# A decoder layer's experts: the down product of four chunks in seven block products instead of eight

## The chip, the cores and the metric

The kernel runs on one core of one Trainium2 chip. The metric is the device time of one execution in microseconds, less is better. Everything is float32 unless said otherwise. The engines are named as the profile names them: PE (TensorE, matrix products), PEld (its weight loads), DVE (VectorE), ACT (ScalarE), POOL (GpSimd) and SP (SyncE, which here only starts DMA transfers).

## The reference, cut to what matters

One decoder layer on x of 4 x 512 tokens and 512 features: attention with 32 query heads, then a product with a quantized context, then a feed-forward part with 8 experts, each step added to x. The change concerns the experts. Each takes its 256 tokens (C) and computes

```python
# E = 8 experts, C = 4*512/8 = 256 tokens each, D = 512, H = 704
h  = silu(einsum('ecd,edh->ech', xd, W1)) * einsum('ecd,edh->ech', xd, W3)
oe = einsum('ech,ehd->ecd', h, W2)          # the "down" product
out = take(oe, ...) * gate                   # rows back to their tokens
return out + silu(xt @ sw1) * (xt @ sw3) @ sw2   # plus a shared expert
```

## The kernel before, in words

The program runs attention, the context product and the shared expert's first part under a planner that mixes jobs between the heads. After that the order is written out by hand: a loop over the 8 experts (L1524), then the last four pieces of the shared expert's down product, with the gathers of the experts' rows and the final additions between them (L1572 to L1591). The change lies in the expert loop and in what it leaves in memory for the end.

H = 704 is cut into five chunks of 128 (HF = 5) and a half chunk of 64. The activations of an expert lie transposed, with H on the partitions, in egTs[e] (the profile calls it slot_s, since it lies in the space of the shared expert's first weights). gT[:, c, :] is chunk c for all 256 tokens, in two tiles of 128 tokens.

One pass of the loop, for expert e:

- Five calls of up7, one for each chunk c. up7 computes the two input products of the chunk at once, as 2 x 2 blocks in seven products (Strassen, in Winograd's form), each of two matmuls 128 x 128 x 128. The products go to PSUM banks, six to the tag "sp" (4 banks, in turn) and product 3 to "av" (1 bank). DVE adds them up (L1345 to L1360), ACT applies Silu (L1359), and POOL makes the last multiplication g = g * c2 (L1361). So a chunk of gT is finished by POOL.
- After each up7, weight_sums puts four additions or subtractions for the next expert's weights on POOL (L1307 to L1310). They are instructions of 256 elements per partition through the helper on L279, as all of POOL's are. After chunk 1 the rows of expert e + 1 are turned (PE and ACT), and after chunk 2 expert_sums puts its four token sums on POOL.
- expert_rest(e + 1): the half chunk of the next expert (one sp bank, L1216, L1231 to L1235).
- down: for each of the two token tiles one bank of tag "mm" (3 banks), a matmul with the half chunk (L1242) and five with the whole chunks (L1253), 512 columns each. With late=True chunk 4 comes last. DVE copies each bank to yo (L1540), and SP writes it to oe.
- Loads on SP in between: rows, weights of expert e + 2, its W2 once down is through (load_w2).

Each engine takes its instructions in the order in which the program issues them. A bank or a buffer is reused in turn: an instruction that writes it waits until the one that read it last is through. c2 and u2 have two buffers each.

Rows of x2 (x after the first two steps) are brought back for the final additions: rows_back (L1519) takes places from a list spare, which starts with the four chunks of h3x[B - 1], the last input of the shared expert, no longer needed. At expert 5 four rows come back into the first four places, and six by xtile into buffers of their own; at expert 7 six more come into places of spare:

```python
    spare = [h3x[B - 1][:, k, :] for k in range(KC)]
        if e == E - 1:
            rows_back(first[2:])
        if e == E - 3:
            rows_back(tiles[0] + first[:2])
            for i in tiles[1] + tiles[2] + tiles[3]:
                xtile(i)
```

## Time and profile before

| what | value |
| --- | --- |
| median of 3 runs | 1563.4 us (1562.38 to 1567.21) |
| profiled execution, its own time | 1567.81 us |
| its span, first to last instruction | 1566.1 us |
| mean granted clock of PE | 0.993 |
| PE busy in the span | 1535.0 us (98%) |
| DVE, ACT, POOL busy | 920.8, 537.4, 544.9 us |
| start of expert 0's first matmul of up7 to the end of expert 7's down | about 1301 to 1523 us |

The profile is of one execution, with times in microseconds from the start of the span. "Busy" of PE includes modelled ends of pipelined matmuls, so two matmuls in a row can overlap in it; the distance of their starts is what one costs. In a timeline line the columns are the start, the duration, the engine, the line of the program, the operation with output and inputs, their sizes and the count; a bracket at the end tells how long the engine stood idle before and what it waited for. In a table by windows the columns are the window, its length, the busy time of PE, PEld, DVE, ACT and POOL with the number of instructions, the granted clock of PE, the DMA share and GB/s. The chain of waits goes back from the last instruction, each step to what released it. A float32 matmul appears as two PE instructions, so the 80 matmuls of the experts' whole chunks are 160 rows on L1253.

### The profile page before, as it was taken

The numbers are of one execution on the slowest core, as the hardware profiler recorded it, in microseconds if no ns is written. First come the engines' busy times: TensorE is split into PE (matmuls) and PEld (weight loads), VectorE is DVE, ScalarE is ACT, GpSimd is POOL, SyncE is SP. The second block draws the span as 40 slices with busy tenths as digits, with TensorE's granted clock in tenths as the row PEclk, the third lists the DMA queues.
The fourth block names the chain that finished last, engine by engine and source line by source line (L and its number), as shares of the span: only waits on it lengthen the run. The fifth ranks groups of instructions, "written<-read, shape, count | busy, mean of one in ns | idle before, by whom it ended". The sixth has DMA issues, their size and how long they took to land.

```text
span 1566.1 us, 22168 instructions
## 1 busy us (share of the span) xinstructions
PE 1535.0 (98%) x7325; PEld 895.8 (57%) x7325; DVE 920.8 (59%) x2732; ACT 537.4 (34%) x1615; POOL 544.9 (35%) x568
## 2 busy tenths in 40 slices
PE   9999999999999999999999999999999999999999
PEld 5455555545545545554555545554446778877864
DVE  4466843467776575887656485665655554434434
ACT  3344443434433434443444444552101121111100
POOL 2131211203334121333312133143535148776723
PEclk9999999999999999999999999999999999999999
DMA  4473431534234344423425342246041234665616
GB/s 150 128 229 133 101 102 28 155 101 102 82 81 142 87 125 135 106 84 79 144 86 131 112 122 62 61 149 202 14 176 68 83 140 147 202 206 200 214 68 215
DMA packets 118227, 193.90 MB, mean 124 GB/s; under 512 B 17120, under 2 KB 36832, under 8 KB 117600
## 3 DMA queue, kind: packets, MB, share of 16 engines
q10 hardware_dynamic: 65216, 100.42, 21.7%
q1 hardware_dynamic: 50336, 83.67, 17.3%
q0 software_dynamic: 2560, 8.39, 1.5%
q8 instruction: 58, 0.95, 0.3%
q14 instruction: 57, 0.47, 0.1%
HBM read 135.54 MB, written 27.53 MB: 104 GB/s over the span
## 4 chain that ended last, share of the span: by engine, by line
PE 86%; DVE 4%; DMA 3%; issue 2%; ACT 2%; POOL 2%; SPq 0%; ACTq 0%; POOLq 0%; DVEq 0%
PE py L414 14%; PE psq L314 13%; PE sc L945 9%; PE av L1026 8%; PE p_e L1336 8%; PE pt L995 8%; PE p_s L1336 5%; PE epy L1253 4%; PE psv L356 4%; PE ys L1253 4%; PE psk L314 3%; ACT pm L978 1%; PE p_s L1216 1%; PE p_e L1216 1%; PE ptr_h L263 1%
## 5 line engine op out<-in xcount | busy, mean ns | idle before, releaser
L978 ACT ACTIVATE pm<-pm,mn 128x256 f32<-128x256 f32 (+3 forms) x512 | 280.9, 550 | 381.8 <-DVE mn L968 356.8
L968 DVE CUSTOM_DVE_ANT_0 pm<-sc,mask 128x256 f32<-128x256 f32 (+3 forms) x512 | 216.6, 485 | 91.6 <-PE sc L945 91.6
L414 PE MATMUL py<-wo,aT 128*128 128x512 f32 x512 | 239.9, 602 | 3.3 <-issue 2.0
L314 PE MATMUL psq<-hT,wq 128*128 128x512 f32 x512 | 236.5, 599 | 2.3 <-DVE y L610 2.3
L279 POOL TENSOR_TENSOR t1q<-t1q,tsq 128x512 f32<-128x512 f32 x64 | 84.2, 1316 | 396.5 <-DMA tsq<-t2q 221.6
L1012 DVE COPY pT<-pt 128x128 f32<-128x128 f32 (+3 forms) x256 | 114.2, 485 | 113.9 <-PE pt L995 105.5
L945 PE MATMUL sc<-kT,t1q 64*128 64x384 f32 (+3 forms) x1024 | 166.7, 450 | 7.3 <-ACT pT L1006 2.5
L995 PEld LDWEIGHTS pt<-ident,pm 128*128 128x128 f32 x1280 | 144.2, 141 | 37.0 <-issue 28.1
L995 PE MATMUL pt<-ident,pm 128*128 128x128 f32 x1280 | 154.9, 274 | 0.3 <-DVE mn L968 0.2
L1026 PE MATMUL av<-pT,v 128*64 128x512 f32 (+3 forms) x1024 | 153.0, 440 | 1.7 <-ACT pT L1006 1.7
L314 PEld LDWEIGHTS psq<-hT,wq 128*128 128x128 f32 x512 | 91.9, 190 | 102.1 <-issue 96.4
L414 PEld LDWEIGHTS py<-wo,aT 128*128 128x128 f32 x512 | 92.1, 190 | 97.2 <-issue 89.2
L1006 ACT COPY pT<-pt 128x128 f32<-128x128 f32 (+3 forms) x256 | 97.1, 430 | 146.6 <-PE pt L995 118.6
L945 PEld LDWEIGHTS sc<-kT,t1q 64*128 64x128 f32 x1024 | 84.5, 187 | 88.5 <-issue 55.6
L279 POOL TENSOR_TENSOR acc<-acc,y 128x512 f32<-128x512 f32 x64 | 81.1, 1271 | 153.5 <-DVE y L610 152.0
L1026 PEld LDWEIGHTS av<-pT,v 128*64 128x64 f32 x1024 | 68.5, 137 | 109.3 <-issue 97.2
L978 ACT ACTIVATION_READ_ACCUMULATOR pm<-pm,mn 128x1 f32 x512 | 95.5, 186 | 0.0
L279 POOL TENSOR_TENSOR aT<-aT,rrb 128x512 f32<-128x512 f32 x64 | 81.8, 1308 | 23.6 <-DMA rrb<-rrd 23.6
L422 DVE TENSOR_TENSOR acc<-py,acc 128x512 f32<-128x512 f32 x64 | 43.8, 686 | 47.3 <-PE py L414 47.0
L1253 PE MATMUL epy<-slot_e,slot_s 128*128 128x512 f32 x160 | 70.8, 597 | 0.0
L323 DVE TENSOR_TENSOR t2q<-psq,rt 128x512 f32<-128x512 f32 x64 | 44.0, 688 | 43.3 <-PE psq L314 40.8
L1253 PE MATMUL ys<-slot_s,gT 128*128 128x512 f32 x140 | 64.4, 610 | 0.0
(245 smaller groups left out, 2078.4 us busy)
## 6 DMA issues: line engine op xcount, KB each, us to landing
slot_e<-in_L_ffn_W_dram SPq DMA_DIRECT2D x14, 1280.0 KB, 8.6
wq<-in_L_attn_wq_dram ACTq DMA_DIRECT2D x16, 1024.0 KB, 6.5
tsq<-t2q SPq DMA_DIRECT2D x256, 64.0 KB, 2.1
wo<-in_L_attn_wo_dram ACTq DMA_DIRECT2D x16, 1024.0 KB, 5.3
rrb<-rrd ACTq DMA_DIRECT2D x32, 512.0 KB, 7.4
slot_e<-in_L_ffn_W_dram SPq DMA_DIRECT2D x7, 1408.0 KB, 6.2
kT<-t1k ACTq DMA_DIRECT2D x64, 128.0 KB, 2.8
wk<-in_L_attn_wk_dram ACTq DMA_DIRECT2D x16, 256.0 KB, 2.9
```

Source lines behind the costliest of these rows:

```text
L279: nc.gpsimd.tensor_tensor(*args)
L314: nc.tensor.matmul(ps, w[:, k, c0 : c0 + P], hTs[b][:, k, :], start=(k == 0), stop=(k == KC - 1),)
L414: nc.tensor.matmul(py, aT[:, r, j * P : (j + 1) * P], wts["o", a][:, r, :], start=(r == 0), stop=(r == 3),)
L945: nc.tensor.matmul(scs[g][:, o : o + nk], qTs[b, p][g * HD : (g + 1) * HD, it * P : nk], kTs[b, p // 2][g * HD : (g + 1) * HD, 0:nk], star ...
L968: nc.vector.tensor_tensor_reduce(out=pm[:, o : o + nk], in0=scs[g][:, o : o + nk], in1=mask[:, T - nk : T], scale=-(HD**-0.5), scalar=3.0e ...
L978: nc.scalar.activation(pm[:, o : o + nk], pm[:, o : o + nk], AF.Exp, bias=mn, scale=-1.0, accum_out=rss[b, a][:, col : col + 1],)
L995: nc.tensor.transpose(pt[:, j * P : (j + 1) * P], pms[g][:, j * P : (j + 1) * P], ident)
L1006: nc.scalar.copy(pT[:, 0 : it + 1, it * P : nk], pt[:, o : o + nk].rearrange("p (j t) -> p j t", t=P),)
L1012: nc.vector.tensor_copy(pT[:, it + 1, 0:nk], pt[:, o : o + nk])
L1026: nc.tensor.matmul(av[g * HD : (g + 1) * HD, j * P : T], vs[b][:, j, v0 : v0 + HD], rhs, start=(j == 0), stop=(j == TB - 1),)
L1253: nc.tensor.matmul(pys[i], gT[:, c, (t + i) * P : (t + i + 1) * P], w2[:, c, :], start=False, stop=(c == HF - 1),)
L1336: nc.tensor.matmul(ps, w[:, k, :], x[:, k, :], start=k == 0, stop=k == 1)
```

## The change

Chunks 0 to 3 of the down product become a 2 x 2 block product: the activations in blocks of (token tile) x (two chunks), W2 in blocks of (two chunks) x (256 columns). Seven products of two matmuls with 256 columns take the place of eight matmuls with 512 columns. The half chunk and chunk 4 stay as they were.

- down_sums: four subtractions on w2 (512 elements per partition each), by DVE, two after chunk 1 and two after chunk 2 of the same expert. The results lie in three chunks of h3x[B - 1]; one replaces a block of w2.
- inner_sums: four additions or subtractions on gT (256 elements each), by DVE. One is issued after chunk 3, three inside up7 of chunk 4, at the second call of mid, which lies between L1352 and L1357 of before. One replaces a block of gT; two results lie in the fourth chunk of h3x[B - 1], one in a tile s4 of its own.
- down7: products 0 to 2 go to sp banks and product 3 to the av bank; products 4 to 6 are added to the mm banks by PE itself. ACT copies product 0, DVE makes four sums of 256 elements, and these are added to the banks where before yo was copied.
- spare no longer holds h3x[B - 1], but four buffers of rows (xes) instead. All ten rows that rows_back brings come at expert 7.

Lines from up7 on are 74 higher in the changed kernel. The whole diff but for blank lines:

```diff
--- before.py
+++ after.py
@@ -1261,6 +1261,80 @@
                 mid()
         return pys
+    def down_sums(w2, ts, which=range(4)):
+        b11, b12, b21, b22 = (
+            w2[:, k : k + 2, c : c + D // 2] for k in (0, 2) for c in (0, D // 2)
+        )
+        t1, t2, t4 = ts
+        todo = (t1, b12, b11), (b12, b22, b12), (t2, b22, t1), (t4, b21, t2)
+        for n in which:
+            nc.vector.tensor_tensor(*todo[n], ALU.subtract)
+        return t1, t2, b12, t4, b11, b21, b22
+    def inner_sums(gT, t, ss, which):
+        a11, a12, a21, a22 = (
+            gT[:, k : k + 2, j * P : (j + 1) * P] for j in (t, t + 1) for k in (0, 2)
+        )
+        s2, s3, s4 = ss
+        todo = (
+            (s3, a11, a21, ALU.subtract), (a21, a21, a22, ALU.add),
+            (s2, a21, a11, ALU.subtract), (s4, a12, s2, ALU.subtract),
+        )
+        for n in which:
+            nc.vector.tensor_tensor(*todo[n])
+        return a11, a12, a21, a22, s2, s3, s4
+    def down7(gT, w2, t, inner, sums, name, tag):
+        a11, a12, s1, a22, s2, s3, s4 = inner
+        t1, t2, t3, t4, b11, b21, b22 = sums
+        half = D // 2
+        pys = [bank(tag, f"{name}_{i}") for i in range(2)]
+        for i, py in enumerate(pys):
+            nc.tensor.matmul(
+                py,
+                gT[i * HT : (i + 1) * HT, HF, (t + i) * P : (t + i + 1) * P],
+                w2[i * HT : (i + 1) * HT, HF, :],
+                start=True,
+                stop=False,
+            )
+        def product(i, a, b, ps=None):
+            first = ps is None
+            if first:
+                ps = bank("av" if i == 3 else "sp", f"d7_{name}_{i}")[:, 0:half]
+            for k in range(2):
+                nc.tensor.matmul(
+                    ps, a[:, k, :], b[:, k, :], start=first and k == 0, stop=first and k == 1
+                )
+            return ps
+        def part(tag, n):
+            return gp.tile([P, n], F32, tag=tag, bufs=2, name=f"d{tag}_{name}")
+        u2, lo, hi = part("u2", half), part("c2", D), part("c2", D)
+        nc.scalar.copy(lo[:, 0:half], product(0, a11, b11))
+        nc.vector.tensor_tensor(u2, product(1, s2, t2), lo[:, 0:half], ALU.add)
+        nc.vector.tensor_tensor(hi[:, 0:half], product(2, s3, t3), u2, ALU.add)
+        p5 = product(3, s1, t1)
+        nc.vector.tensor_tensor(lo[:, half:D], p5, u2, ALU.add)
+        nc.vector.tensor_tensor(hi[:, half:D], p5, hi[:, 0:half], ALU.add)
+        product(4, a12, b21, pys[0][:, 0:half])
+        product(5, s4, b22, pys[0][:, half:D])
+        product(6, a22, t4, pys[1][:, 0:half])
+        for i, (py, more) in enumerate(zip(pys, (lo, hi))):
+            nc.tensor.matmul(
+                py,
+                gT[:, HF - 1, (t + i) * P : (t + i + 1) * P],
+                w2[:, HF - 1, :],
+                start=False,
+                stop=True,
+            )
+            yield py, more
     def down_last(gT, w2, t, name):
         parts = [(0, 0, D), (1, 0, D // 2), (1, D // 2, D)]
@@ -1512,7 +1586,9 @@
     for pair in tiles:
         kept.update(pair)
     first = [i for i in range(NT) if i not in kept]
-    spare = [h3x[B - 1][:, k, :] for k in range(KC)]
+    spare = []
     spare += [xSs.rearrange("p i k t -> p (i k t)")[:, k * D : (k + 1) * D] for k in range(4)]
     spare += [wS_flat[:, k * D : (k + 1) * D] for k in range(NHC * CAP // D)]
@@ -1521,9 +1597,23 @@
             xts[i] = spare.pop(0)
             nc.sync.dma_start(out=xts[i], in_=x2[i * P : (i + 1) * P, :])
+    h3v = h3x[B - 1]
+    ts = [h3v[:, k, :].rearrange("p (k c) -> p k c", k=2) for k in range(3)]
+    ss = [h3v[:, 3, k * 2 * P : (k + 1) * 2 * P].rearrange("p (k t) -> p k t", k=2) for k in range(2)]
+    s4 = ep.tile([P, 2, P], F32, name="s4")
+    ss.append(s4)
     for e in range(E):
         for c in range(HF):
-            up7(evw[e][0], exS[e], egTs[e][:, c, :], c, CAP, f"e{e}_{c}")
+            def mid(ns=0, room=0, calls=[]):
+                calls.append(room)
+                if c == HF - 1 and len(calls) == 2:
+                    inner_sums(egTs[e], 0, ss, (1, 2, 3))
+            up7(evw[e][0], exS[e], egTs[e][:, c, :], c, CAP, f"e{e}_{c}", mid)
+            if c in (1, 2):
+                down_sums(evw[e][1], ts, (0, 1) if c == 1 else (2, 3))
+            if c == 3:
+                inner_sums(egTs[e], 0, ss, (0,))
             if e < E - 1:
                 weight_sums(evw[e + 1][0], c)
             if c == 1:
@@ -1534,16 +1624,17 @@
         expert_rest(e + 1)
         load_e(e + 2)
         if e == E - 1:
-            rows_back(first[2:])
-        for t, py in enumerate(down(egTs[e], evw[e][1], 0, f"epy_{e}", "mm", late=True)):
+            spare.extend(xes[e, t] for t in range(CT) for e in (E - 2, E - 1))
+            rows_back(tiles[0] + first)
+        inner, sums = inner_sums(egTs[e], 0, ss, ()), down_sums(evw[e][1], ts, ())
+        for t, (py, more) in enumerate(down7(egTs[e], evw[e][1], 0, inner, sums, f"epy_{e}", "mm")):
             yo = ep.tile([P, D], F32, tag="yo", bufs=2, name=f"yo_{e}_{t}")
-            nc.vector.tensor_copy(yo, py)
+            nc.vector.tensor_tensor(yo, py, more, ALU.add)
             r0 = e * CAP + t * P
             nc.sync.dma_start(out=oe[r0 : r0 + P, :], in_=yo)
         load_w2(e + 2)
         if e == E - 3:
-            rows_back(tiles[0] + first[:2])
             for i in tiles[1] + tiles[2] + tiles[3]:
                 xtile(i)
```

## The prediction

> **What bounds the kernel now.** I read the page's busy shares first, then the chain that ended last, then the timeline of one expert. Expert 4 stands for all; in what follows *t* is the time in us after its first matmul at 1413.63.

> ```profile
> PE 1535.0 (98%) x7325; PEld 895.8 (57%) x7325; DVE 920.8 (59%) x2732; ACT 537.4 (34%) x1615; POOL 544.9 (35%) x568
> ```

> ```profile
> 1405.01 8.78 PE epy L1253 x20
> 1413.79 6.25 PE p_e L1336 x56
> 1420.91 9.38 PE p_e L1336 x84
> 1433.08 8.78 PE epy L1253 x20
> 1441.86 6.25 PE p_e L1336 x56
> ```

> The chain through the experts consists of PE's matmuls alone, one expert each 28.07 us (1441.86 - 1413.79). So a matmul less is time gained, and anything that keeps PE waiting is time lost. DVE has slack here (14.6 to 18.3 us busy in 40). POOL has less: the timeline shows it in one unbroken run of 29 instructions from t=4.05 (1417.68) to t=25.9, and late against the others:

> ```profile
> 1429.48 0.28 DVE L1352 TENSOR_TENSOR slot_s<-p_e,p_e 128x128 f32<-128x128 f32 x1
> ...
> 1429.88 0.29 DVE L1357 TENSOR_TENSOR slot_s<-p_e,u_e 128x128 f32<-128x128 f32 x1
> ...
> 1431.22 0.73 POOL L279 TENSOR_TENSOR xS<-h3x,xS 128x256 f32<-128x256 f32 x1
> 1431.91 0.73 POOL L279 TENSOR_TENSOR slot_s<-slot_s,c_e 128x256 f32<-128x256 f32 x1
> 1431.95 1.13 PE L1242 MATMUL epy<-slot_e,slot_s 64*128 64x512 f32 x4
> ...
> 1432.59 0.73 POOL L279 TENSOR_TENSOR wS<-slot_e 128x256 f32<-128x256 f32 x1
> ```

> The slot_s product at 1431.91 is the one that finishes chunk 3 of gT (t=18.3 to 19.0). DVE is by then through chunk 4 (L1352 at t=15.9, L1357 at t=16.3). Before the change nobody suffers: `down` takes chunk 3 as its fourth matmul.

> [...]

> ```profile
> 1261.06 0.68 DVE L1320 TENSOR_TENSOR xS<-h3x 128x512 f32<-128x512 f32 x1
> 1261.66 1.75 DVE L1320 TENSOR_TENSOR xS<-h3x,xS 128x512 f32<-128x512 f32 x1
> ...
> 1261.17 1.70 POOL L279 TENSOR_TENSOR gT<-gT,c_s 128x512 f32<-128x512 f32 x1 [7.59 <-DVE xS L1320]
> ```

> POOL takes 1.70 instead of its usual 1.31; the last DVE subtraction takes 1.75 instead of 0.69 and ends 0.54 after POOL does. [...]

> ```profile
> 1283.85 1.94 PE L263 MATMUL ptr_e<-ident,xe 128*128 128x128 f32 x8 [3.21 <-DMA xe<-xd]
> ...
> 1283.00:1286.00 3.00, 2.15 (x9) 2.10 (x10) 0.00 (x0) 0.76 (x2) 2.84 (x5) 0.50 0.92 312
> 1286.00:1289.00 3.00, 3.00 (x9) 2.37 (x7) 0.00 (x0) 0.79 (x2) 2.92 (x4) 0.50 1.02 375
> 1289.00:1292.00 3.00, 3.00 (x14) 2.63 (x13) 1.60 (x4) 0.00 (x0) 2.77 (x5) 0.92 1.04 371
> ```

> The seventh figure after the window is the clock (the five bracketed busy times come first). A wait of 3.21 us was followed by 5.6 us of work at half clock (1283.85 to 1289.5), 2.8 us lost. The other long PE waits: 3.08 us at 1163.9 cost (1170.0 - 1167.0)/2 = 1.5 us; waits of 2.00 (586) and 1.47 (352 and 1134) were also each followed by 3.4 us at 0.50; 1.70 (1070) and 1.37 (914) were not.

> **The change part by part.**

> *Matmuls removed.* A 128x512 matmul is two PE instructions 0.427 apart (20 take 8.78 with their tail). Those of 128x256 with the same kind of operands (p_s, L1336) start 0.865 apart in fours, 0.216 each. Per expert 16 instructions of 0.427 (6.83) become 28 of 0.216 (6.03): **-0.80 us**, eight times. The half chunk (L1242) and chunk 4 stay. Weight loads of 0.19 remain under 0.216.

> *Sums of w2 (T1 to T4).* Four DVE instructions of 512 elements, both inputs in SBUF, two after chunk 1 (t=6.7) and two after chunk 2 (t=10.7). Alone 0.69 each; but POOL is in its run, so they alternate with it. At 376 to 383 four POOL products (usual 1.27) alternate with DVE's L460 and L462, which take 1.64 each and start 1.68 apart: a DVE instruction takes 1.68 - 1.27 = 0.41 from POOL. So T1 to T4 make POOL late by 4 x 0.41 = 1.64. DVE itself: two of them behind a POOL instruction each last about 2 us; chunk 2's L1345 (t=8.3) comes 0.5 late, chunk 3's (t=11.4) 1.2 late, at 12.65 to 12.95. It frees the bank of product 1 for product 6 (six `sp` banks' worth per chunk on four banks), due at t=12.8: PE waits about **0.2**. Bounds 0 and 1.

> *Sums of gT.* S3 after chunk 3: 256 elements, alone 0.42, takes 0.15 more from POOL. S1, S2, S4 stand in DVE's queue between L1352 and L1357 of chunk 4, at t=16.2, and S1 needs POOL's product of chunk 3. That now ends at 19.0 + 1.64 + 0.15 = 20.8. POOL goes straight on with its weight sums; S1, S2 and S4 each get in behind one of them. The hold of a 256 POOL instruction is about 0.60 (0.73 less the 0.13 to 0.15 by which the other starts before its end), that of a DVE one 0.27 (half the 0.54 above). S1 starts at 21.4 and ends at 21.85, S2 at 22.7, S4 at 23.6; L1357 and its semaphore end at 23.95.

> *Who waits.* Behind these three on DVE: L1357 and L1360 of chunk 4, the two of `expert_rest` (L1234, L1235) and the first sums of `down7`; behind L1357 on ACT: the Silu of chunk 4, that of the rest and the copy of product 0. On PE: product 1 needs S2 and the bank that L1357 frees (chunk 4's products 4, 5, 6 and the rest fill all four; product 0 takes the one that L1352 freed). PE comes to it at t = 19.4 (start of L1253 now) + 0.2 + 0.86 (product 0) = 20.45. It waits until 23.95: **+3.5**. Bounds: no sharing of the port at all gives 19.0 + 3 x 0.42 + 0.29 = 20.6, a wait of 0.2; a full POOL instruction and a full DVE one per step (1.15 instead of 0.87), and the upper end for the T sums, gives about 4.8.

> *Clock.* A wait of 3.5 is of the kind that led to half clock both times (3.08, 3.21): (1.5 + 2.8)/2 = **+2.1**. Bounds 0 and 2.8.

> *The rest of down7.* `hi` takes the c2 buffer of chunk 4, so its first sum waits for POOL's product of chunk 4 (24.4 to 25.1: after Silu at 24.35); PE ends product 2 at 25.7, so that is covered. The ACT copy ends near 25. Three more DVE sums of 0.42 lie under products 4 to 6 (2.6 us) and chunk 4 (1.7 us). yo's addition reads PSUM and SBUF at the price of the copy (0.69 for 128x512, as L1396): nothing. If the cover goes, each costs 0.4.

> *Rows.* Four loads of x2 (256 KB each) move from expert 5 to expert 7 on SP, 10 instead of 6 ahead of the writes of yo; at 0.43 each to issue from 1512.4 they are out by 1517, and yo comes at 1523. If transfers lag, the gathers (1527 to 1547) shift by at most 2 to 3; the DVE work behind them is over some 6 us before PE needs a bank. Nothing, at most 2. Of POOL's and ACT's queues only the copy is new.

> *Sum.* Experts 0 to 6: -0.80 + 0.2 + 3.5 + 2.1 = +5.0 each. Expert 7 has no weight sums on POOL (its chunk 3 is ready 1 us before S1 is issued): -0.8. Total 7 x 5.0 - 0.8 = +34.2. The profiled run took 1567.8 (span 1566.1), 4.4 above the median of 1563.4; the difference is laid on the median: **1597.6**, rounded 1597.

> **The rivals.** *Clock kept*: the wait comes[...]. 7 x (0.2 + 3.5 - 0.8) - 0.8 = +19.5: 1583. For it: one wait of 1.70 left the clock alone; against: both above 3 did not. *The port costs nothing (ends faster)*: 256-element instructions slip into the gaps of 0.08 between POOL's (0.73 long, 0.81 apart in part), POOL isn't pushed back, S1 starts at 19.05 and PE waits 0.2: 8 x -0.8 + 7 x 0.2 = -5.0: 1558. It decides where product 1 can start before t = 19.4 + 0.86 + 0.8 = 21.05; later than that the saving is gone. [...] *Worse*: the upper bounds together, 7 x (-0.8 + 0.2 + 4.8 + 2.8) - 0.8 = +48: 1612. That the matmuls are not saved is excluded: 14 of 256 columns stand for 8 of 512 in the program.

> **How the numbers follow.** Stall and half clock 0.60 (1588 to 1607), clock kept 0.18 (1573 to 1588), free port 0.15 (1556 to 1564), worse 0.07. The range 1570 to 1612 leaves out the free port and half of the worst. About 0.3% (4.7 us) is what a measurement of this kernel can tell from no change: the free port splits into 0.08 faster and 0.07 within; the rest, 0.85, is slower.

> **What would show it.** Right: PE idle of 3 to 4 us per expert ahead of product 1, released by DVE; S1's line idle for POOL; DVE's subtractions of 512 at 1.0 or more instead of 0.69; POOL's product of chunk 3 near t=20.8; a clock of 0.50 for 3 us or more after it; expert 7 faster by 0.8. Wrong: S1, S2, S4 at 0.42 back to back, PE idle below 0.5 per expert, or a period of the experts under 28.

## The result, and the profile after

The changed kernel takes **1583.99 us** (median of 5 runs, 1580.02 to 1587.52) where the kernel before takes 1564.04 (5 runs, 1562.38 to 1567.21): ratio **1.0129** (95% interval 1.0115 to 1.0144), 20 us slower. The profiled execution took 1580.02 with a span of 1578.2. The predicted 1597 is 13 us too high: the direction, the place and the wait behind POOL are as predicted, the half clock behind that wait is not.

The page of after, its busy times and the shares of the chain that ended last; below them the shares of before:

```profile
PE 1531.1 (97%) x7421; PEld 914.5 (58%) x7421; DVE 983.0 (62%) x2828; ACT 539.1 (34%) x1623; POOL 557.6 (35%) x568
...
PE 79%; POOL 8%; DVE 6%; DMA 3%; issue 2%; ACT 2%; SPq 0%; ACTq 0%; POOLq 0%; DVEq 0%
```

```profile
PE 86%; DVE 4%; DMA 3%; issue 2%; ACT 2%; POOL 2%; SPq 0%; ACTq 0%; POOLq 0%; DVEq 0%
```

PE has less work and still the program takes longer. The chain tells why: before, PE held 86% of it and POOL and DVE 6%; now these two hold 14%. POOL has as many instructions as before (568) and 12.7 us more of busy time: they are the same operations, and those that run beside DVE's new ones are slower (next to the second pair of w2 sums 1.06 and 1.17 us instead of 0.73).

What the chain passes through in one expert, the fourth (the chain of after, start, length, what). The experts are numbered from 0, so this is expert 3:

```profile
1387.41 5.82 PE p_e L1410 x52
...
1404.05 0.69 POOL xS L279
1404.74 0.07 issue
1404.81 0.79 POOL xS L279 x2
1405.60 0.58 issue
1406.18 0.72 POOL xS L279
1406.90 0.69 POOL slot_s L279
1407.60 0.02 issue
1407.62 0.94 DVE slot_s L1286
1408.56 0.02 issue
1408.58 0.84 DVE h3x L1286
1409.42 0.02 issue
1409.45 0.83 DVE s L1286
1410.28 0.21 DVE slot_s L1431
1410.49 0.04 issue
1410.53 2.86 PE d_epy L1310 x12
```

Read it from below. Product 1 of down7 (L1310, 1410.53) starts when DVE's L1431 has freed its bank. L1431 stands in DVE's queue behind S1, S2 and S4 (the three L1286). S1 starts when POOL has finished chunk 3 of gT (the slot_s of L279, 1406.90). And that multiplication comes at the end of POOL's run, right behind four token sums for the next expert (xS), which nobody needs yet.

What PE and DVE wait for there (timeline of after):

```profile
1406.86 0.73 POOL L279 TENSOR_TENSOR slot_s<-slot_s,c_e 128x256 f32<-128x256 f32 x1
1407.47 1.13 PE L1310 MATMUL d_epy<-slot_e,slot_s 128*128 128x256 f32 x4
1407.62 0.93 DVE L1286 TENSOR_TENSOR slot_s<-slot_s 128x256 f32<-128x256 f32 x1 [3.44 <-POOL slot_s L279]
1408.35 0.78 POOL L279 TENSOR_TENSOR slot_e<-slot_e 128x256 f32<-128x256 f32 x1
1408.58 0.83 DVE L1286 TENSOR_TENSOR h3x<-slot_s 128x256 f32<-128x256 f32 x1
1409.21 0.79 POOL L279 TENSOR_TENSOR wS<-slot_e 128x256 f32<-128x256 f32 x1
1409.45 0.83 DVE L1286 TENSOR_TENSOR s<-slot_s,h3x 128x256 f32<-128x256 f32 x1
...
1410.20 0.28 DVE L1431 TENSOR_TENSOR slot_s<-p_e,u_e 128x128 f32<-128x128 f32 x1
1410.53 1.13 PE L1310 MATMUL d_epy<-h3x 128*128 128x256 f32 x4 [1.93 <-DVE slot_s L1431]
```

DVE stood idle for 3.44 us with its next work behind S1; S1, S2 and S4 take 0.93, 0.83 and 0.83 instead of the 0.41 to 0.42 of such a sum alone, in strict turn with POOL; and PE waits 1.93 for product 1.

An expert as a whole, expert 4 before and expert 3 after, from its first matmul to the next expert's (windows: length, then busy time and count of PE, PEld, DVE, ACT and POOL, clock, DMA share, GB/s):

```profile
1413.63:1441.70 28.07, 28.07 (x181) 22.04 (x180) 11.42 (x40) 4.77 (x13) 20.58 (x29) 1.00 0.58 198
```

```profile
1387.25:1417.53 30.28, 28.02 (x193) 24.39 (x192) 19.54 (x52) 5.03 (x14) 22.43 (x29) 1.00 0.57 183
```

In what follows the length of such a window is called the period: 28.07 before, 30.28 after (30.40 in expert 0, 32.01 in expert 4); for expert 7, which prepares nothing, 25.56 before and 25.39 after. The loop takes 222.1 us before (1301.33 to 1523.41) and 239.2 after (1296.28 to 1535.50), 17.1 more. The end of the program behind it is 42.7 us in both. Ahead of the loop, where the program is the same, the two executions differ by 5 us the other way, so their own times (1567.81 and 1580.02) show only 12.2 of it.

### The profile page after: what moved, and what is told of

It reads as the page before. It is cut to its first block, busy times and chain, and to the rows that moved or that the text cites. A ratio compares the mean times of both kernels' runs of the same rounds, so it can differ in the third digit from the quotient of the medians.

```text
span 1578.2 us, 22472 instructions
## 1 busy us (share of the span) xinstructions
PE 1531.1 (97%) x7421; PEld 914.5 (58%) x7421; DVE 983.0 (62%) x2828; ACT 539.1 (34%) x1623; POOL 557.6 (35%) x568
## 4 chain that ended last, share of the span: by engine, by line
PE 79%; POOL 8%; DVE 6%; DMA 3%; issue 2%; ACT 2%; SPq 0%; ACTq 0%; POOLq 0%; DVEq 0%
PE py L414 14%; PE psq L314 13%; PE sc L945 9%; PE av L1026 8%; PE pt L995 8%; PE p_s L1410 5%; PE psv L356 4%; PE ys L1253 3%; PE psk L314 3%; PE p_e L1410 3%; POOL wS L279 3%; PE d_epy L1310 2%; POOL slot_s L279 1%; PE epy L1310 1%; PE p_s L1216 1%
## 5 line engine op out<-in xcount | busy, mean ns | idle before, releaser
L279 POOL TENSOR_TENSOR t1q<-t1q,tsq 128x512 f32<-128x512 f32 x64 | 83.8, 1310 | 395.8 <-DMA tsq<-t2q 241.7
L279 POOL TENSOR_TENSOR acc<-acc,y 128x512 f32<-128x512 f32 x64 | 81.1, 1272 | 151.3 <-DVE y L610 149.8
L279 POOL TENSOR_TENSOR aT<-aT,rrb 128x512 f32<-128x512 f32 x64 | 81.9, 1312 | 25.3 <-DMA rrb<-rrd 25.3
L610 DVE TENSOR_TENSOR y<-py,sxw 128x512 f32<-128x512 f32 x64 | 43.4, 687 | 35.2 <-PE py L608 22.3
L1433 ACT ACTIVATE slot_s<-slot_s 128x256 f32<-128x256 f32 x40 | 16.7, 417 | 140.9 <-DVE slot_s L1431 140.9
```

The lines of the kernel that those rows point to most:

```text
L279: nc.gpsimd.tensor_tensor(*args)
```

## The experiments

Theory: product 1 is late because POOL finishes chunk 3 late and DVE's queue stands behind S1; the w2 sums add to it, since POOL's instructions beside them take longer. "The port" in the prediction and in the expectations is a name for this: DVE's and POOL's instructions slow each other. The runs show it by their durations (0.83 instead of 0.42 us for S2, 1.06 and 1.17 instead of 0.73 on POOL); what the two share isn't shown. Rivals: the w2 sums on DVE are the whole loss; or the half clock behind the wait is most of it. The ratios are to the kernel before, run on the same chip (its medians: 1565.08 for e1 to e4, 1565.05 for e5 to e8, 1563.96 for e9 and e10). Edits are to the changed kernel unless said otherwise.

### e1: S1 without POOL's chunk

```diff
-            (s3, a11, a21, ALU.subtract), (a21, a21, a22, ALU.add),
+            (s3, a11, a21, ALU.subtract), (a21, a21, a11, ALU.add),
```

> Leaves out the true S1: it adds block a11 (chunks 0 and 1) where a22 (chunks 2 and 3) belongs, so that S1 no longer waits for POOL's product of chunk 3; everything else is as in the changed kernel. Theory (DVE's queue stands still behind S1 until POOL finishes chunk 3): S1, S2, S4 run at t=16.6 to 19.3 behind POOL's instructions, the last bank is free at t=19.6, before PE wants it (21.1). The PE wait of about 2.2 per expert ahead of product 1 goes, and with it the half clock: 7 x 2.2 + about 4 = 19 less, 1565 (1562 to 1569). What stays is 0.85 of delay in chunks 2 to 4. Rival 1 (the three sums cost through the port, not through the wait): they still run beside POOL, so 1580 or more. Rival 2 (the seven products themselves are dearer than eight): 1580 or more.

Measured: 1572.16 us (7 runs), ratio 1.0034 (1.0022 to 1.0047), period 28.80. About three quarters of the loss is gone. I had expected all of it (1562 to 1569), so this missed. What was left (timeline of e1):

```profile
1407.17 0.93 DVE L1286 TENSOR_TENSOR s<-slot_s,h3x 128x256 f32<-128x256 f32 x1 [1.98 <-POOL slot_s L279]
...
1408.36 1.13 PE L1310 MATMUL d_epy<-h3x 128*128 128x256 f32 x4 [0.46 <-DVE slot_s L1431]
```

S4 = a12 - S2 reads chunk 3 too (it is in a12). I had overlooked that: the wait moved from S1 to S4, and S1 and S2 alone were taken out of it. e9 takes away both.

### e2: POOL's sums for the next expert behind chunk 3

```diff
-            if e < E - 1:
-                weight_sums(evw[e + 1][0], c)
+            if e < E - 1 and c != 2:
+                for k in (2, 3) if c == 3 else (c,):
+                    weight_sums(evw[e + 1][0], k)
...
-            if c == 2:
+            if c == 3:
                 expert_sums(e + 1)
```

> Same results as the changed kernel; POOL's order alone changes: the weight sums of chunk 2 and the token sums (8 instructions of 0.73, some 5.9 us) come after the product of chunk 3 instead of ahead of it. Theory: the product of chunk 3 ends near t=15.5 instead of 20.3, S1 follows chunk 4's fourth sum at once, no PE wait at product 1: 1565 (1561 to 1569), as in the kernel whose S1 doesn't wait. PE wait left: the delays of chunks 2 to 4 (0.85 per expert). If POOL now ends too late (its run reaches beyond t=28), the next expert's product of chunk 0 is late instead, and the gain is below half. Rival (port alone): 1580 or more[...].

Measured: 1564.51 (20 runs), ratio 0.9996 (0.9987 to 1.0006), period 28.07, in experts 0, 4 and 6 27.51 to 27.57. The whole computation is done and the loss is gone. POOL's product of chunk 3 is in time, and S1 finds its input ready (timeline of e2):

```profile
1422.44 0.73 POOL L279 TENSOR_TENSOR slot_s<-slot_s,c_e 128x256 f32<-128x256 f32 x1 [0.84 <-DVE h3x L1286]
...
1424.13 0.80 DVE L1286 TENSOR_TENSOR slot_s<-slot_s 128x256 f32<-128x256 f32 x1
...
1428.46 1.03 PE L1310 MATMUL d_epy<-h3x 128*128 128x256 f32 x4
```

No bracket on S1 and none on product 1. S1, S2 and S4 still cost 0.80 to 0.83 each; that is harmless when they start in time. But nothing is won over the kernel before, though the matmuls saved are worth 0.8 an expert: something else takes them back.

### e3: the w2 sums made once

```diff
+    down_sums(evw[0][1], ts)
     for e in range(E):
...
-            if c in (1, 2):
-                down_sums(evw[e][1], ts, (0, 1) if c == 1 else (2, 3))
```

> Leaves out the four sums of w2 in each expert (they are made once, before expert 0, so the products take old sums); the sums of gT and their wait stay. Theory (each DVE sum with two SBUF inputs also pushes POOL back and chunks 2 to 4 with it): POOL's product of chunk 3 ends at t=19.2 instead of 20.3, the delay of PE in chunks 2 to 4 falls from 0.85 to 0.1, expert 7 gains 0.6; product 1 starts at t=22.1 instead of 23.2. 7 x 1.1 + 0.6 = 8 less, and fewer half clocks (the wait is 1.75 instead of 2.2): 1572 to 1577. Rival (only POOL's order counts, the port is free): within 2 of 1584.

Measured: 1575.32 (4 runs), ratio 1.0058 (1.0041 to 1.0075), period 28.71, 1.57 less than after. It is the sum of two things: PE isn't held up in chunks 3 and 4 (0.85, below), and chunk 3 comes earlier, so that the wait for product 1 shrinks from 1.93 to 1.19. The wait remains, so the w2 sums are not the whole loss. The time holds one wait more: PE stands 3.0 us in expert 0, behind the four sums that are now made just ahead of it.

### e4: the wait filled with matmuls

```diff
+        if fill:
+            pt = bank("av", f"fill_{name}")
+            for _ in range(fill):
+                nc.tensor.transpose(pt[:, 0:P], ident, ident)
```

It stands between product 0 and product 1, with fill = 16 in experts 0 to 6.

> The changed kernel with 16 transposes of the identity (about 0.11 each, 1.8 in all) on PE between product 0 and product 1 of experts 0 to 6, in the wait of 2.2; nobody reads them. Theory on the clock (the changed kernel's runs differ, 1580 to 1587, by how many of the 7 waits lead to a half clock of 3.4, 1.7 lost each): no half clock in the experts, mean clock at 0.995 or above in all runs, times within 3 of each other at 1577 to 1581. Rival (the spread is something else, and the clock costs nothing in the median): 1584, or up to 4 more if the transposes are in the way.

Measured: 1578.25 (4 runs), ratio 1.0076 (1.0059 to 1.0093), period 30.29 to 30.31 in five experts, 30.42 and 30.47 in experts 0 and 4. The wait is as long, but PE is busy for most of it: the 16 transposes take 1.91 us, and 0.20 to 0.22 stay idle in five experts, 0.90 and 0.89 in experts 0 and 4. No expert of the profiled execution has the half clock; product 1 takes 1.13 in each of the seven. The mean granted clocks say the same of all runs: 0.996 to 0.999 here, 0.991 to 0.995 in the five runs of after. The four times differ by 4.4, where I had expected 3 at most. So of the 20 us some 15 are the longer periods themselves (7 x 2.21 - 0.17 = 15.3), and the clock has the rest: 4.7 by this sum, (1.0129 - 1.0076) x 1565 = 8.3 by the two ratios. That is 0.7 to 1.2 us an expert. The second figure is the weaker one: e4 lies 0.0076 x 1565 = 11.9 above before, some 3.5 less than the longer periods alone come to, so with four runs this comparison is uncertain by about that much.

### e5: the token sums alone behind chunk 3

```diff
-            if c == 2:
+            if c == 3:
                 expert_sums(e + 1)
```

> Same results as the changed kernel; only the token sums (4 of POOL's instructions, 2.9 us) move from ahead of the product of chunk 3 to after it, half of what the kernel with the other POOL order moves. Theory (PE's wait is what POOL's lateness leaves over): the product of chunk 3 ends at t=20.3 - 2.9 = 17.4, S1, S2, S4 and the sum that frees the bank end 2.9 later, at t=20.3, still ahead of PE (21.1): no wait at product 1, period 28.1 as there, 1565 (1562 to 1568). Rival (the gain there came from fewer clashes on the port): half the gain, 1574.

Measured: 1563.56 (20 runs), ratio 0.9988 (0.9979 to 0.9996), period 28.07 (27.55 and 27.59 in experts 0 and 4). Four POOL instructions of 0.73 in the wrong place are enough for the whole stall: no wait at product 1 is left. The weight sums of chunk 2 need not move.

### e6: S1, S2 and S4 one call of mid later

```diff
-                if c == HF - 1 and len(calls) == 2:
+                if c == HF - 1 and len(calls) == 3:
```

> Same results; POOL's order is that of the changed kernel, and S1, S2, S4 are issued after chunk 4's last DVE sum instead of between its fifth and sixth. Theory (two causes hold product 1: the data S2, and the bank that chunk 4's sixth sum frees, which stands behind S4): the banks are free at once, S2 ends at t=22.1, where the bank was free at 23.2. PE's wait at product 1 falls from 2.2 to about 1.1, period 30.28 to 29.2, 7 x 1.1 = 7.7 less and fewer half clocks: 1573 (1570 to 1577). If the bank alone held it: no wait, 1565. If the data alone: 1582 or more.

Measured: 1572.67 (12 runs), ratio 1.0048 (1.0035 to 1.0061), period 29.21. Now L1431 and L1434 stand ahead of S1, and the bank is free in time; product 1 waits for its own operand instead (timeline and waits of e6; in the waits the total, the count and the longest, us):

```profile
1349.74 1.13 PE L1310 MATMUL d_epy<-h3x 128*128 128x256 f32 x4 [0.88 <-DVE h3x L1286]
```

```profile
PE d_epy L1310 <- DVE h3x L1286: 7.5, 7, 1.6
```

The wait goes from 1.93 to 0.88: S4 and L1431 are no longer in front of it, but S2 is the end of the same chain. So the place in DVE's queue makes half of the stall. It does so only because POOL is late: with POOL in time (e2, e5) neither half is there, and the sums stand where they stood.

### e7: the kernel before with four subtractions of w2

To the kernel before, with the rows moved as in the changed kernel. Nothing uses the results, and the one that replaces a block of w2 goes to a buffer instead.

```diff
+            if c in (1, 2):
+                down_sums(evw[e][1], ts, (0, 1) if c == 1 else (2, 3))
```

> The kernel before with four DVE subtractions of 512 elements on w2 in each expert, where the changed kernel has them, into the space of the last input, which nobody reads (none in place); rows come back as in the changed kernel. No block products, no sums of gT. Theory on the port: period up by 0.75 (the delay in chunks 2 to 4), POOL later by 1.1 without anybody waiting: 8 x 0.75 = +6 against the kernel before, 1571 (1569 to 1573). Rival (DVE has slack, so its sums cost PE nothing): 1565.

Measured: 1570.03 (20 runs), ratio 1.0031 (1.0021 to 1.0041), period 28.89 (+0.82) in five experts, 28.33 and 28.39 in experts 0 and 4, and 26.21 in expert 7 (+0.65). So in most experts the w2 sums alone cost as much as the products save. The table of waits shows only 1.0 us of it for all experts; the rest is seen from the starts (timeline of e7, PE):

```profile
1429.30 0.61 PE L1347 MATMUL p_e<-xS,slot_e 128*128 128x128 f32 x4
1429.75 0.61 PE L1347 MATMUL p_e<-h3x,slot_e 128*128 128x128 f32 x4
1430.44 1.13 PE L1347 MATMUL p_e<-xS,wS 128*128 128x128 f32 x8
```

The second group comes 0.45 after the first, as always, and the third 0.69 after the second. No bracket stands there: a group is shown as 0.61 long although the next can start 0.45 after it, and that overlap of 0.16 hides most of the 0.24 lost.

### e8: the w2 sums one at a time, with e2's order on POOL

To e2's kernel: one subtraction at the start of the expert and one after each of chunks 0, 1 and 2.

```diff
     for e in range(E):
+        down_sums(evw[e][1], ts, (0,))
...
-            if c in (1, 2):
-                down_sums(evw[e][1], ts, (0, 1) if c == 1 else (2, 3))
+            if c < 3:
+                down_sums(evw[e][1], ts, (c + 1,))
```

> Same results as the changed kernel; POOL's order as in the second experiment, and the four sums of w2 one by one: at the start of the expert, and after chunks 0, 1 and 2. Theory (a DVE sum with two SBUF inputs takes about 1.1 beside POOL, as much as DVE has left in a chunk: 3.1 less seven sums of 0.29; two in a row are too much): the delay in chunks 2 to 4 falls from 0.85 to 0.2 or less, period 27.3 to 27.5 against 28.07 before, and 1560 (1557 to 1562), faster than both kernels by 4 or more against before. If the second sum in a row isn't the cause: 1564 as there.

Measured: **1558.93** (6 runs), ratio **0.9955** (0.9939 to 0.997). It does the whole computation and is faster than both kernels. An expert of it, by its window:

```profile
1382.89:1410.14 27.25, 27.25 (x193) 24.32 (x192) 18.09 (x52) 5.14 (x14) 21.90 (x30) 1.00 0.62 203
```

The period is 28.07 - 0.82, PE is busy throughout, and expert 7 takes 24.74 (25.56 - 0.82). Only expert 0 gains less, with 27.69. Seven times 0.82 and 0.38 are 6.1, and the medians differ by 6.1. That 0.82 is the price of the removed matmuls, measured without anything that hides it.

### e9: neither S1 nor S4 reads chunk 3

```diff
-            (s3, a11, a21, ALU.subtract), (a21, a21, a22, ALU.add),
-            (s2, a21, a11, ALU.subtract), (s4, a12, s2, ALU.subtract),
+            (s3, a11, a21, ALU.subtract), (a21, a21, a11, ALU.add),
+            (s2, a21, a11, ALU.subtract), (s4, a11, s2, ALU.subtract),
```

> Leaves out the true S1 and the true S4: both take block a11 (chunks 0 and 1) where a22 and a12 (chunks 2 and 3) belong, so that none of DVE's sums waits for POOL's product of chunk 3. The first experiment freed S1 alone; S4 also reads chunk 3, and its period was 28.80 instead of 28.07. Theory (that remainder is S4's wait on the same product): no PE wait at product 1, period 28.07 as with the other POOL order, 1565 (1562 to 1567). Rival (the remainder is the three sums' own time beside POOL): period 28.8, 1572 as there.

Measured: 1563.46 (12 runs), ratio 0.9989 (0.9972 to 1.0005), period 28.07. POOL's order is that of after, its sums as many, S1, S2 and S4 are there with their places and sizes; only the wait for chunk 3 is taken away, and the stall is gone (waits of e9, PE, all of the loop):

```profile
PE p_e L1410 <- DVE u_e L1419: 1.0, 5, 0.2
```

The remainder of e1 was S4's wait. And as in e2, what is left of the change is about zero: 0.8 saved, up to 0.8 for the w2 sums.

### e10: the w2 sums one at a time, POOL's order as in after

The second half of e8's edit, without e2's.

> Same results as the changed kernel, with POOL's order as there; only the four sums of w2 are spread, one at the start of the expert and one after each of chunks 0, 1 and 2. Theory (PE's time at product 1 is set by POOL's product of chunk 3, so a delay of PE ahead of it is hidden in the wait): chunks 2 to 4 are on time again, but PE only waits longer at product 1; the period falls just by what POOL is pushed back less, from 30.28 to 29.8 (29.5 to 30.2), and the half clocks stay: 1580 (1577 to 1584). Rival (the two delays add up, as their sizes do in the sum of the prediction): period 29.5 or less, 1577 or less.

Measured: 1584.63 (4 runs), ratio 1.0125 (1.0091 to 1.016): the improvement that is worth 0.82 an expert in e8 is worth nothing here. Without the half clock the period is 29.87, 0.41 less than after; the rest of the 0.82 comes back as a longer wait, since POOL is as late as ever and PE is there earlier. And in every second expert the clock is halved behind that wait, with periods of 31.44 to 31.54 (timeline of e10, two experts in a row, product 1):

```profile
1385.71 1.13 PE L1310 MATMUL d_epy<-h3x 128*128 128x256 f32 x4 [2.35 <-DVE slot_s L1431]
...
1415.59 2.08 PE L1310 MATMUL d_epy<-h3x 128*128 128x256 f32 x4 [2.35 <-DVE slot_s L1431]
```

The same wait, and once the product takes 1.13 and once 2.08. The period at full clock is as expected. The time is 4.6 us above the 1580 that I expected, just outside the range, and that stays open in part: the three long periods cost 3 x 1.6 = 4.9 us, but the 1580 already held as much half clock as after has. The loop is 239.3 us long, 17.3 more than before, while the medians differ by 20.7; so some 3 us of the difference, with four runs, lie outside the loop, where the program is the same.

## Why the prediction was right, and which terms were off

**Matmuls removed: right.** -0.80 predicted, -0.82 in e8, in seven of eight experts.

**POOL and the port: right, slightly too dear.** Chunk 3 was to be finished at t=20.8 instead of 19.0; it was at 20.3 (1407.59 - 1387.25). I took 0.41 of POOL's time for each w2 sum. The pair after chunk 2 shows POOL's rows next to them at 1.06 and 1.17 instead of 0.73, which is 0.77 for two sums, 0.38 each, and less in the distance of their starts. The turns of S1, S2 and S4 with POOL were to be 0.87 apart; they started at 1407.62, 1408.58 and 1409.45, 0.96 and 0.87 apart. In after the price for DVE's sums with both inputs in SBUF was 0.83 instead of 0.42 for 256 elements (L1286) and mostly 1.10 instead of 0.68 for 512 (L1272); its sums of 128 elements that read PSUM took 0.28 to 0.29 beside POOL's run in before, and as much in expert 7, where POOL has no such run. The rival *the port costs nothing* fell by these rows.

**Delay of chunks 2 to 4: mis-sized, 0.2 predicted, 0.85 measured.** I found the right bank, but only the first of two waits, and too short. PE's starts in chunks 3 and 4 (timeline of after):

```profile
1399.73 0.61 PE L1410 MATMUL p_e<-h3x,wS 128*128 128x128 f32 x4
1400.56 0.71 PE L1410 MATMUL p_e<-xS,slot_e 128*128 128x128 f32 x4 [0.21 <-DVE u_e L1419]
1401.10 0.61 PE L1410 MATMUL p_e<-h3x,slot_e 128*128 128x128 f32 x4
1401.83 1.13 PE L1410 MATMUL p_e<-xS,wS 128*128 128x128 f32 x8
```

Groups of four start 0.45 apart when nothing is in the way. Here chunk 3's last product comes 0.83 after the one before it (+0.38), then 0.54 (+0.09), and chunk 4's second product 0.73 after its first (+0.28). The bracket admits 0.21. DVE's two w2 sums lasted 2.39 us together (1397.91 to 1400.30) and chunk 3's sums began behind them; the four banks of sp pass the delay on to the next chunk. In experts 0 and 4 the same two sums took only 1.81 and 1.88, and the delay is about 0.3 there (e7); why these two differ is open. e7 measures this term alone, at 0.82, and by it the w2 sums also take back most of what I gave expert 7: -0.8 predicted, -0.17 measured.

**The wait for product 1: right in cause, mis-sized, 3.5 predicted, 2.2 measured.** Both ends of it moved towards each other. PE reaches product 1 at t=21.1 instead of 20.45: 0.6 later, because of the delay just told. L1431 is through at t=23.2 instead of 23.95: 0.7 earlier, because POOL lost less. By starts it is 1410.53 - 1407.47 - 0.86 = 2.2; the table of waits gives 15.0 us for seven experts, 1.93 to 1.95 in five and 2.63 and 2.62 in experts 0 and 4, where PE comes earlier:

```profile
PE d_epy L1310 <- DVE slot_s L1431: 15.0, 7, 2.6
PE p_e L1410 <- DVE u_e L1419: 1.0, 5, 0.2
```

The sum per expert is -0.80 + 0.85 + 2.2 = 2.25, against 30.28 - 28.07 = 2.21 measured.

**Clock: the step that failed.** +2.1 predicted for each of seven experts, because I took every such wait to lead to half clock, at the price of the two waits above 3 us that I knew. The waits that came were shorter, and in the profiled execution one of seven led to half clock; what seven waits of 3.5 would have done, no run shows. That execution is the fastest of the five; the others have lower clocks (timeline and windows of after; the figure after the five busy times is the clock):

```profile
1319.67 1.13 PE L1310 MATMUL d_epy<-h3x 128*128 128x256 f32 x4 [2.63 <-DVE slot_s L1431]
...
1440.99 2.08 PE L1310 MATMUL d_epy<-h3x 128*128 128x256 f32 x4 [2.62 <-DVE slot_s L1431]
```

```profile
1314.45:1317.86 3.41, 2.60 (x11) 1.05 (x9) 1.06 (x2) 0.00 (x0) 3.33 (x6) 1.00 1.01 400
1317.86:1321.28 3.42, 1.60 (x7) 1.44 (x8) 2.65 (x7) 1.17 (x3) 3.12 (x5) 1.00 1.04 390
1321.28:1324.69 3.41, 3.41 (x17) 3.01 (x16) 1.46 (x4) 0.00 (x0) 2.47 (x4) 1.00 0.13 29
...
1437.33:1440.74 3.41, 1.04 (x4) 0.58 (x4) 2.58 (x4) 0.00 (x0) 3.17 (x6) 1.00 1.03 406
1440.74:1444.16 3.42, 3.17 (x8) 2.55 (x9) 1.41 (x5) 1.17 (x3) 3.12 (x5) 0.50 0.68 234
1444.16:1447.57 3.41, 3.41 (x17) 3.02 (x16) 1.18 (x3) 0.00 (x0) 1.05 (x2) 1.00 0.01 2
```

3.4 us at 0.50, 1.7 us lost, a period of 32.01 instead of 30.28; the other wait of the same length cost nothing beyond itself. The windows are laid on the edges of the half clock, in steps of 3.41 us. The wait at 1440.99 falls almost whole into one of them (PE busy 1.04 of 3.41 us), the one at 1319.67 across two (2.60 and 1.60). Averaged over the runs the half clock cost 0.7 to 1.2 us an expert (e4). So the result is in the range, but below the likeliest case (1588 to 1607) and at the rival *clock kept* (1583), which I had given 0.18. That its 1583 fits to 1 us is luck: it was summed from a wait of 3.5 and no half clock, and what came is a wait of 2.2, 0.65 more of delay and some half clock. 13 us is what the prediction has too much, and 7 x 2.1 = 14.7 less the 5 to 8 that the clock did cost is 7 to 10 of it. The shorter wait has another 7 x 1.3 = 9, and the longer delay with expert 7 takes back 7 x 0.65 + 0.6 = 5.

**The rest of down7 and the rows: right.** hi's first sum waits 3.22 us for POOL in e2 and PE doesn't notice. The end of the program is as long as before with all ten rows at expert 7.

## What to carry to other kernels

Before a step is put on an engine, look at which engine writes its input last and what that engine does just ahead of it: here four sums for the next expert, 2.9 us on POOL, stood in front of one multiplication that had just become urgent, and moving them undid the whole stall (e5). In after DVE stood idle for 3.44 us on S1 with L1431, whose bank PE needed, issued behind it; so count who stands behind an instruction that waits. And when a saving disappears, price the helpers beside it alone (e7): the w2 sums ate about what the products gave until they were spread one to a chunk, and that in turn was worth something only with the stall gone (e8 against e10).
